# An attention kernel with image prompts: x turned by VectorE instead of TensorE, and another order of loads on SyncE's queue

## The chip, the core and the metric

The kernel runs on one core of one Trainium2 chip. A core has TensorE (PE) for matmuls, whose results go to eight PSUM banks, VectorE (DVE), ScalarE (ACT), GpSimd (POOL), and SyncE (SP), which here does nothing but issue DMAs, one after the other in program order. Sixteen DMA engines carry them. All data are float32. The metric is the time of one execution on the device in microseconds (us); the median of some timed executions stands for a kernel.

## The reference, cut to what matters

```python
# x (8, 112, 320), ehs (8, 375, 512): the last 4 tokens of ehs are image prompts
text_ehs, ip_ehs = ehs[:, :-4], ehs[:, -4:]              # 371 and 4 tokens
q, k_t, v_t = heads(x @ W_q), heads(text_ehs @ W_k), heads(text_ehs @ W_v)   # 20 heads of 16
probs_t  = softmax(einsum('bhsd,bhtd->bhst', q, k_t) * scale)
text_out = einsum('bhst,bhtd->bhsd', probs_t, v_t)
qsem = l2norm(einsum('bhst,bte->bhse', probs_t, text_ehs))     # wide: 512 per head
sem  = einsum('bhse,bne->bhsn', qsem, l2norm(ip_ehs))
fused = einsum('bhsd,bhnd->bhsn', q, heads(ip_ehs @ W_k_ip)) * scale + 0.5 * sem
probs_ip = softmax(fused) * smask[:, None]
out = (text_out + einsum('bhsn,bhnd->bhsd', probs_ip, heads(ip_ehs @ W_v_ip))) @ W_out + b_out + x
```

## The kernel before, in words

The 8 batches have 20 heads each, taken in 5 groups of 4. A step (b, g) is one group of one batch, and 40 steps follow one another, (0,0) to (7,4); a loop (L1207 on) writes out 35 of them, and the last batch has its own loop. `qsem` is never formed: its norm comes from a Gram matrix of the context, so that one product of the probabilities with a matrix `u` (Gram matrix, values and prompt columns side by side) gives all that a head needs.

One step of the main loop, by engine:

- PE: `multiplied` (L735 to 756), 96 matmuls with 32 contraction rows, probabilities against `u`, into four PSUM banks `ps_qd`, one for each head (L748). Between them stand the scores of the step two ahead (L686): two heads before the first matmul ("now") and two at the seventh row tile ("then"). The step is filled up by `between(b, g)` (L1079 to 1129): the next batch's Gram matrix (L502), values (L578) and keys (L544), queries (L315 to 358), and the projection of the finished batch (`ps_a` L950, `ps_o` L962).
- DVE: the maximum of each score row (L709), the transposition of the probabilities for the next step, 128x1536, from xg to xgT (`transposed`, L729), the context's transposition ct to ctxT (L404, three of 128x512 per batch), and `reduced` (L794), which multiplies `ps_qd` by the probabilities and sums; it reads a bank last, so the next step's matmuls into that bank wait for it.
- ACT: the exponential (L712), the copies of prompt logits (L714), of value sums (L761), and those of keys (L540, L551) and values from PSUM.
- POOL: the u of the next step from `vr` (L655) and smaller products.
- SP: the queue of DMAs. Each of the four heads' probabilities goes from p to xg, 162.3 KB (`sent`, L721); the Gram matrix goes to u in twelve pieces (`gram_to_groups`, L520), the values through DRAM to vr (L594, L603). Bulk loads stand in the same queue: the context of batch b+3 at the end of step (b,4) (`load_next`; four blocks of 176.0 KB, L140, and four rests of 9.5 KB, L145), the prompt values vip at the same place (L611, 560 KB), x as kept for the residual, x_sb, in three loads at the ends of steps (0,0), (1,0) and (2,0) (L1178), w_out at (0,2), and a copy of prompt values by head from DRAM to DRAM, vipx, at (5,1) (L618). The issue of a DMA waits until the engine's data are ready and until the eighth DMA before it has landed, as eight semaphores go round.

Queries are made for one batch (0), for pairs (1 and 2, 3 and 4, 5 and 6) and for one (7). `project_queries` turns x (112 x 320 per batch) by three PE transposes per batch (L333) into PSUM, ACT copies them to xT (L336), nine matmuls with wq follow in three pieces (L344), and DVE multiplies them by a mask into qm (L353). The transposes of a pair are run as one block at (0,1), (1,3), (3,3) and (5,3), the three pieces of matmuls in later steps. In the last step before a pair's turn, `turned` makes the "now" scores come after the first block's start, since they need the new qm.

Of the kernel before, what the change touches and what calls it, by code (L numbers as in the profile page):

```python
# [8 lines left out]
F32 = mybir.dt.float32  # L9
# [11 lines left out]
def kernel(  # L21
# [76 lines left out]

    x_sb = const.tile([S, B, C], F32, tag="x_sb", name="x_sb")
    wq_sb = const.tile([P, NC, CP], F32, tag="wq_sb", name="wq_sb")  # L100
    wk_sb = const.tile([P, NE, CP], F32, tag="wk_sb", name="wk_sb")
# [9 lines left out]
    sm_sb = const.tile([S, 1], F32, tag="sm_sb", name="sm_sb")  # L111
    bias_sb = const.tile([S, C], F32, tag="bias_sb", name="bias_sb")

    def load_channels(eng, t, w):
# [14 lines left out]
    def chunk(t, e):  # L129
        return t.rearrange("t (p e) -> t e p", e=NE)[:, e, :]  # L130

    def load_ctx(b):
        ct = io.tile([P, NT, E], F32, tag="ct", name=f"ct_{b}")
        if b >= LEAD:

            v = ct.rearrange("p c e -> p (c e)").rearrange("p (j f) -> p j f", f=P)
            full = TT // RG
            nc.gpsimd.memset(v[:, full, :], 0.0)
            for a in range(QN):
                nc.sync.dma_start(  # L140
                    v[a * RG : (a + 1) * RG, :full, :],
                    ehs[b, : full * RG, a * P : (a + 1) * P].rearrange("(j i) f -> i j f", i=RG),
                )
            for a in range(QN):
                nc.sync.dma_start(  # L145
                    v[a * RG : a * RG + TT - full * RG, full, :],
                    ehs[b, full * RG : TT, a * P : (a + 1) * P],
                )
            return v
# [8 lines left out]
    loaded = {0: load_ctx(0)}  # L158
    nc.scalar.dma_start(ip_sb, ehs[:, TT:, :])

# [154 lines left out]
    def project_queries(bs):  # L315
        n = len(bs)
        end = bs[0] == B - 1
        xT = work.tile([P, NC, 2 * S], F32, tag="xT", name=f"xT_{bs[0]}", bufs=1)
# [5 lines left out]
        nc.gpsimd.memset(xT[REST:, FULL, :], 0.0)  # L324
        for i in range(NC):
            cn = min(P, C - i * P)
            if bs[0] == 0:

                ps = ps_qd.tile([P, 512], F32, tag="qd", name=f"ps_x_0_{i}")
            else:  # L330
                ps = bank(f"ps_x_{bs[0]}_{i}", spare=i > 0)
            for j, b in enumerate(bs):
                nc.tensor.transpose(  # L333
                    ps[:cn, j * S : (j + 1) * S], x_sb[:, b, i * P : i * P + cn], ident[:S, :S]
                )
            nc.scalar.copy(xT[:cn, i, : n * S], ps[:cn, : n * S])  # L336
            yield
        for i in range(NC):
# [4 lines left out]
            for j in range(NC):  # L343
                nc.tensor.matmul(  # L344
                    ps[:, : n * S],
                    wq_sb[:, j, i * P : (i + 1) * P],
                    xT[:, j, : n * S],
                    start=(j == 0),
                    stop=(j == NC - 1),
                )  # L350
# [164 lines left out]

    def gram_to_groups(b, blocks, eng=nc.sync):

        for q in blocks:
            for a in range(GROUP):
                eng.dma_start(  # L520
                    st[b]["u"][a * RG : (a + 1) * RG, q * GW : (q + 1) * GW],
                    ug[q * RG : (q + 1) * RG, :],
                )
# [411 lines left out]
    def prompt_sums_and_projection(b, s, eng, part, n, h0, i0, i1, w, attn, ah):  # L935
# [11 lines left out]

        ps = bank(f"ps_a_{b}_{h0}")
        for i in range(i0, i1):
# [129 lines left out]
    def between(b, g):  # L1079
# [16 lines left out]
        if g == 1:  # L1096
            if new:
                run(("v", nb), lambda: values(nb), 1 if b == 0 else 2)
            if b == 0:
                run(("pp",), prompt_projections)  # L1100
            for bs in first if b == 0 else ():
                run(("q", bs[0]), lambda: project_queries(bs), 3)
        if g == 2 and new:
# [6 lines left out]
        if g == 3:  # L1110
            if new:
                run(("k", nb), None, 1)
            if b > 0 and new:
                run(("f", b - 1), None)
            for bs in first if b > 0 else ():
                run(("q", bs[0]), lambda: project_queries(bs), 3)
            for bs in rest:
                run(("q", bs[0]), None)
        if g < NT and nb + 1 < B:
            run(("c", nb + 1), lambda: transposed_context(nb + 1))  # L1120
        if g == 4:
            if b > 0 and new:
# [3 lines left out]
            for bs in (first if b > 0 else []) + (rest if b < B - 2 else []):  # L1126
                run(("q", bs[0]), None)
            if b == 0:
                run(("t", b), lambda: prompt_logits(b))

# [22 lines left out]
    nc.gpsimd.tensor_copy(wv_sb[:, :, C:], wk_sb[:, :, FULL * P : C])  # L1153
    spread(nc.gpsimd, wk_sb)
    run(("q", 0), None)
    run(("k", 0), lambda: keys(0))
# [4 lines left out]
    drain(transposed_context(1))  # L1161
    run(("q", 0), None)
    run(("k", 0), None)
    for a in range(GROUP):
# [15 lines left out]
    def load_rest(n):  # L1180

        if n == 0:
            load_x(1, 3)
        elif n == 2:
            load_channels(nc.sync, wo_sb, w_out)
        elif n == 3:
            nc.sync.dma_start(sm_sb, smask.unsqueeze(1))
            nc.sync.dma_start(bias_sb, b_out.partition_broadcast(S))
        elif n == NG:
            load_x(3, 5)  # L1190
        elif n == 2 * NG:
            load_x(5, B)


    def ahead(n):
# [11 lines left out]
    for n, (b, g) in enumerate(steps[:-NG]):  # L1207
        now, more, then = ahead(n)
        turned = (b, g) == (0, 2) or g == NG - 1 and any(bs[0] == b + 2 for bs in pairs)
        if not turned:  # L1210
            for c, a in now:
                scores(*c, a)
                probabilities(*c, a)
        for j, _ in enumerate(multiplied(b, g)):
            if j == 0:
                for c, a in now if turned else ():
                    scores(*c, a)
# [7 lines left out]
            if j == 2:  # L1225
# [5 lines left out]
                if 1 <= g <= 3:  # L1231
                    gram_to_groups(b + 1, {1: (0,), 2: (2,), 3: (3,)}[g])

# [173 lines left out]
```

## Time and profile before

| | us |
|---|---|
| median of 3 timed executions | 427.46 (427.1 to 427.54) |
| the profiled execution, its own time | 429.28 |
| its span, first to last instruction | 427.6 |

| engine | busy, share of the span |
|---|---|
| ACT | 188.7 us, 44% |
| POOL | 110.9 us, 26% |
| DMA queue of SP and ACT | 58.5% of 16 engines' time, 62.42 MB |

The profile is that of one execution. A row of the timeline has the start in us from the span's start, the duration (of a row "xN", of N like instructions from the first start to the last end), engine, line, operation, output and input tile, and in brackets how long the engine had been idle before and what released it. A row of the waits has engine, tile and line of the instruction that waited, what it waited for, and then us in total, times, and the longest. A row of a line's forms has the least, median and greatest duration in ns.

### The profile page before, as it was taken

To read this page: it belongs to the slowest core of one execution; us is meant where nothing else is said; L and a number is where in the kernel's file an instruction comes from. 1 tells how busy PE (TensorE), PEld (TensorE's weight loads), DVE (VectorE), ACT (ScalarE), POOL (GpSimd) and SP (SyncE) were. 2 spreads that over 40 slices of the span, in tenths; PEclk is the share of its full clock that TensorE was granted. 3 is DMA by queue.
4 is the path that set the end of the run, shared out by engine and by line. 5 is a ranking of instruction groups with operands and counts; after the bars stand their busy time and mean duration, and the time that the engine had idled before them with its cause. 6 is when DMAs were issued, how large, how long until landed. Compare 5 with 4: busy or idle time off the path is not lost.

```text
span 427.6 us, 13996 instructions
## 1 busy us (share of the span) xinstructions
PE 417.4 (98%) x5521; PEld 326.8 (76%) x5521; DVE 327.4 (77%) x672; ACT 188.7 (44%) x659; POOL 110.9 (26%) x275
## 2 busy tenths in 40 slices
PE   7999999999999999999999999999999999999995
PEld 7867767887767867788777877779776987777993
DVE  5038569887987869897896979797877887888873
ACT  2344342245433443436335363334533373446773
POOL 5310101112061112511151120611143120505550
PEclk9999999999999999999999999999999999999999
DMA  8677665687655956567556956458556537564200
GB/s 252 189 191 210 152 159 156 161 203 150 163 142 140 204 136 175 142 145 173 151 136 140 189 124 186 132 130 177 140 165 149 151 102 184 148 151 116 69 3 27
DMA packets 57631, 64.28 MB, mean 150 GB/s; under 512 B 18448, under 2 KB 51592, under 8 KB 57566
## 3 DMA queue, kind: packets, MB, share of 16 engines
q1 hardware_dynamic: 56934, 62.42, 58.5%
q8 instruction: 44, 0.72, 0.8%
q10 hardware_dynamic: 632, 0.96, 0.7%
q14 instruction: 21, 0.17, 0.1%
HBM read 18.67 MB, written 5.32 MB: 56 GB/s over the span
## 4 chain that ended last, share of the span: by engine, by line
PE 83%; DMA 5%; DVE 5%; ACT 4%; issue 1%; SPq 1%; POOL 0%; DVEq 0%; ACTq 0%
PE ps_qd L748 36%; PE ps_v L578 12%; PE ps_k L544 9%; PE ps_s L686 9%; PE ps_g L502 6%; PE ps_q L344 3%; DMA xg<-p 3%; PE ps_o L962 3%; DMA vipx<-vipd 2%; DVE xgT L729 1%; PE ps_g L458 1%; ACT p L712 1%; ACT shared L787 1%; DMA ip_sb<-in_ctx_dram 1%; PE ps_x L333 1%
## 5 line engine op out<-in xcount | busy, mean ns | idle before, releaser
L748 PE MATMUL ps_qd<-u,xgT 32*112 32x168 f32 (+11 forms) x3840 | 219.9, 351 | 0.3 <-POOL u L655 0.3
L748 PEld LDWEIGHTS ps_qd<-u,xgT 32*112 32x112 f32 x3840 | 187.2, 172 | 27.1 <-DVE ss L794 1.3
L729 DVE STREAM_TRANSPOSE xgT<-xg 128x1536 f32<-128x1536 f32 (+1 forms) x45 | 119.5, 2674 | 18.2 <-DMA xg<-p 17.5
L712 ACT ACTIVATE p<-ps_s,nmx 112x371 f32<-112x371 f32 x156 | 85.2, 587 | 65.9 <-DVE nmx L709 45.2
L709 DVE TENSOR_REDUCE nmx<-ps_s 112x1 f32<-112x371 f32 x160 | 77.2, 527 | 26.6 <-PE ps_s L686 24.6
L794 DVE CUSTOM_DVE_ANT_0 junk<-ps_qd,p 112x371 f32<-112x371 f32 x146 | 79.3, 543 | 17.9 <-PE ps_qd L748 1.4
L686 PE MATMUL ps_s<-kT,qm 32*112 32x375 f32 (+1 forms) x320 | 66.4, 496 | 0.7 <-DVE qm L353 0.6
L655 POOL COPY u<-vr 128x64 f32<-128x64 f32 x120 | 26.0, 238 | 149.9 <-PE ps_qd L748 99.2
L578 PE MATMUL ps_v<-wv_sb,ctxT 128*128 128x384 f32 (+1 forms) x192 | 63.0, 477 | 0.0
L578 PEld LDWEIGHTS ps_v<-wv_sb,ctxT 128*128 128x128 f32 x192 | 35.7, 190 | 20.9
L761 ACT COPY pvs<-ps_qd 112x21 f32<-112x21 f32 x151 | 16.3, 190 | 74.4 <-PE ps_qd L748 74.1
L544 PE MATMUL ps_k<-ctxT,wk_sb 128*128 128x371 f32 x136 | 46.9, 488 | 0.2 <-DVE ctxT L425 0.2
L544 PEld LDWEIGHTS ps_k<-ctxT,wk_sb 128*128 128x128 f32 x136 | 24.4, 189 | 14.0 <-issue 0.5
L686 PEld LDWEIGHTS ps_s<-kT,qm 32*112 32x112 f32 x320 | 23.8, 170 | 12.7 <-issue 10.3
L502 PE MATMUL ps_g<-ctxT 128*32 128x375 f32 (+11 forms) x672 | 30.4, 333 | 0.0
L502 PEld LDWEIGHTS ps_g<-ctxT 128*32 128x32 f32 x672 | 27.7, 110 | 2.0
L585 ACT COPY vext<-ps_v 128x384 f32<-128x384 f32 (+1 forms) x24 | 11.3, 471 | 31.9 <-PE ps_v L578 31.8
L353 DVE TENSOR_SCALAR qm<-ps_q,emask 128x224 f32<-128x224 f32 (+1 forms) x25 | 9.0, 395 | 20.3 <-PE ps_q L344 20.2
L714 ACT COPY ipl<-ps_s 112x4 f32<-112x4 f32 x140 | 24.4, 174 | 0.0
L937 POOL TENSOR_TENSOR wv<-vip,w 112x1280 f32<-112x1280 f32 x6 | 14.8, 2470 | 28.2 <-DVE w L877 28.2
L404 DVE STREAM_TRANSPOSE ctxT<-ct 128x512 f32<-128x512 f32 x18 | 20.1, 1119 | 1.8 <-DMA ct<-in_ctx_dram 1.8
L475 POOL TENSOR_TENSOR ug<-ug,half 128x128 f32<-128x128 f32 (+1 forms) x24 | 10.5, 449 | 32.1 <-ACT ug L474 32.1
(171 smaller groups left out, 320.2 us busy)
## 6 DMA issues: line engine op xcount, KB each, us to landing
xg<-p SPq DMA_DIRECT2D x156, 162.3 KB
u<-ug SPq DMA_DIRECT2D x124, 99.0 KB
ct<-in_ctx_dram SPq DMA_DIRECT2D x24, 176.0 KB
vr<-vd SPq DMA_DIRECT2D x32, 120.0 KB
vip<-vipd SPq DMA_DIRECT2D x6, 560.0 KB
vd<-vext SPq DMA_DIRECT2D x7, 320.0 KB
vd<-vext SPq DMA_DIRECT2D x7, 160.0 KB
out_dram<-ob SPq DMA_DIRECT2D x8, 140.0 KB
```

The lines of the kernel that those rows point to most:

```text
L404: nc.vector.transpose(ctxT[:, :, c * P : (c + 1) * P].rearrange("p e (j i) -> p j e i", i=RG), ct[:, some, :].rearrange("p j (k e) -> p j ...
L502: nc.tensor.matmul(ps[c][q * RG : (q + 1) * RG, j * RG - c * P : T - c * P], ctxT[:, e, j * RG : (j + 1) * RG], ctxT[:, e, j * RG : T], st ...
L544: nc.tensor.matmul(ps[:, :TT], wk_sb[:, e, i * P : (i + 1) * P], s["ctxT"][:, e, :TT], start=(e == 0), stop=(e == NE - 1),)
L578: nc.tensor.matmul(ps[:, :w], ctxT[:, e, c * P : (c + 1) * P], wv_sb[:, e, :w], start=(e == 0), stop=(e == NE - 1),)
L655: nc.gpsimd.tensor_copy(v, dealt(b, c, s["vr"][:, c * QN : (c + 1) * QN, g, :]))
L686: nc.tensor.matmul(ps[:S, :w], qm[a * RG : (a + 1) * RG, i, r, j * S : (j + 1) * S], s["kT"][a * RG : (a + 1) * RG, i, :w], start=True, st ...
L709: nc.vector.tensor_reduce(nmx, ps[:S, :TT], AX.X, ALU.max, negate=True)
L712: nc.scalar.activation(s["p", g][:, a, :], ps[:S, :TT], AF.Exp, bias=nmx)
L714: nc.scalar.copy(s["ipl"][:, groups[g][a], :], ps[:S, TT:T])
L729: nc.vector.transpose(xT[:, j : j + n].rearrange("p j (k q) -> p q j k", q=QN), xg[:, :, j * RG : (j + n) * RG].rearrange("p q (j k) -> p ...
L748: nc.tensor.matmul(banks[a][:S, j * RG : UW], xT[a * RG : (a + 1) * RG, j, :S], region(b, c)[a * RG : (a + 1) * RG, q, j * RG - c * P :], ...
L794: nc.vector.tensor_tensor_reduce(out=junk, in0=ps[:S, :TT], in1=s["p", g][:, a, :], scale=1.0, scalar=0.0, op0=ALU.mult, op1=ALU.add, accu ...
```

## The change

It touches what turns x, and where loads stand in SP's queue.

- x of batches 1 to 7 is loaded a second time, in blocks (xr_sb; four DMAs per batch, each 28 partitions with 4 pieces of 320 bytes), and turned by DVE: three stream transposes per batch over a stride of 5 columns, straight into xT. PE transposes and ACT copies stay for batch 0. The channels come out in another order, so wq is loaded a second time, in the prologue behind batch 0's queries, in row order (p c) instead of (c p), and spread again.
- x is turned at (0,0) and (0,1) for batches 1 and 2, and at (1,2), (1,3), (3,2), (3,3), (5,2) for the others, after that step's reductions and context transposition. The context transposes of batch 2 move from (0,0), (0,1), (0,2) to (0,1), (0,2), (0,3).
- `turned` goes; only at (0,3) do the "now" scores come behind the first block (`late`). The transposed heads of odd batches get a bank of the scores' pool; prompt_logits of batch 0 moves from behind (0,4) to behind its value sums.
- Loads: context 2 moves from the prologue to the end of (0,0); 3 and 4 stay; 5, 6 and 7 move from the ends of (2,4), (3,4), (4,4) into (2,0), (3,0), (4,0), blocks between the "now" and the "then" probabilities, rests behind the "then" ones. x_sb is loaded batch by batch at (b,4). The blocks xr stand at the ends of (0,0) and (1,0), between the probabilities of (1,0), and in (2,4) and (4,4). w_out goes to (1,1), vipx to (6,0). The pieces of u go in halves, spread over the middles and ends of steps (b,1), (b,2), (b,3).

```diff
+    def load_pairs(eng, t, w):
+        w = w.rearrange("(p c) f -> p c f", c=5)
+        eng.dma_start(t[0::2, :, :C], w[:, :3, :])
+        eng.dma_start(t[1::2, :2, :C], w[:, 3:, :])
+
+    def load_x_blocks(b, j):
+        for a in range(QN):
+            nc.sync.dma_start(
+                xr_sb[a * RG : a * RG + S // QN, j, :, :XB],
+                x[b, :, a * XB : (a + 1) * XB].rearrange("(q i) f -> i q f", q=QN),
+            )
...
+        for j in range(n if qT is None else 0):
+            for e in range(NC):
+                nc.vector.transpose(
+                    xT[:, e, j],
+                    xr_sb[:, j, :, e : e + XB]
+                    .rearrange("p q (m c) -> p q m c", c=5)[:, :, :, 0:4:3],
+                )
             yield
...
-        ps = bank(f"ps_a_{b}_{h0}")
+        ps = bank(f"ps_a_{b}_{h0}", spare=b % 2 == 1)
...
-        if g < NT and nb + 1 < B:
+        if nb + 1 < B and g in ((1, 2, 3) if b == 0 else (0, 1, 2)):
             run(("c", nb + 1), lambda: transposed_context(nb + 1))
+        for bs in first:
+            if g in ((0, 1) if b == 0 else (2, 3)[: len(bs)]):
+                run(("q", bs[0]), lambda: project_queries(bs))
...
+    nc.gpsimd.memset(wq_sb[:, FULL, :], 0.0)
+    load_pairs(nc.sync, wq_sb, w_q)
+    load_x_blocks(1, 0)
     run(("k", 0), None)
...
-    load_next(2)
...
+    spread(nc.gpsimd, wq_sb)
     prologue.close()
...
-        if n == 0:
-            load_x(1, 3)
-        elif n == 2:
-            load_channels(nc.sync, wo_sb, w_out)
-        elif n == 3:
+        if n == 3:
...
-        elif n == NG:
-            load_x(3, 5)
-        elif n == 2 * NG:
-            load_x(5, B)
+        elif n == NG + 1:
+            load_channels(nc.sync, wo_sb, w_out)
+        if g == NG - 1:
+            load_x(b, b + 1 if b < B - 2 else B)
+    x_loads = {
+        (0, 0): ((0, 0), (2, 1)),
+        (1, 0): ((3, 0), (4, 1)),
+        (2, NG - 1): ((5, 0), (6, 1)),
+        (4, NG - 1): ((7, 0),),
+    }
...
-        turned = (b, g) == (0, 2) or g == NG - 1 and any(bs[0] == b + 2 for bs in pairs)
-        if not turned:
+        late = (b, g) == (0, NG - 2)
...
                 if 1 <= g <= 3:
-                    gram_to_groups(b + 1, {1: (0,), 2: (2,), 3: (3,)}[g])
+                    gram_to_groups(b + 1, {1: (0,), 2: (1,), 3: (3,)}[g], parts=halves[g == 2])
+                elif g == 0 and 2 <= b < B - 3:
+                    load_ctx_blocks(b + 3)
+                for c, i in x_loads.get((b, g), ())[: int(n > 0)]:
+                    load_x_blocks(c, i)
...
+        if n == NG - 1:
+            run(("t", b), lambda: prompt_logits(b))
...
-        if g == NG - 1:
+        if n == 0:
+            load_next(2)
+        elif g == NG - 1 and b < 2:
             load_next(b + 3)
+        elif g == 0 and 2 <= b < B - 3:
+            load_ctx_rest(b + 3)
+        for c, i in x_loads.get((b, g), ())[1:]:
+            load_x_blocks(c, i)
         if g == 1:
-            gram_to_groups(b + 1, (1,))
+            gram_to_groups(b + 1, (0,), parts=halves[1])
+            gram_to_groups(b + 1, (1,), parts=halves[0])
+        elif g == 2:
+            gram_to_groups(b + 1, (2,))
         elif g == 3:
+            gram_to_groups(b + 1, (3,), parts=halves[1])
             values_to_groups(b + 1)
...
-        if (b, g) == (B - 3, 1):
+        if (b, g) == (B - 2, 0):
             prompt_values_by_head()
```

More of the change, by code (lines that the diff above doesn't have):

```diff
@@ L514, in gram, with gram_to_groups @@
             yield
-    def gram_to_groups(b, blocks, eng=nc.sync):
+    def gram_to_groups(b, blocks, eng=nc.sync, parts=range(GROUP)):
         for q in blocks:
-            for a in range(GROUP):
+            for a in parts:
                 eng.dma_start(
@@ L1154 @@
     spread(nc.gpsimd, wk_sb)
+    nc.gpsimd.memset(xr_sb, 0.0)
     run(("q", 0), None)
@@ L1180, in load_rest @@
     def load_rest(n):
[L1182 to L1186 removed]
+        if n == 3:
             nc.sync.dma_start(sm_sb, smask.unsqueeze(1))
             nc.sync.dma_start(bias_sb, b_out.partition_broadcast(S))
[L1189 to L1192 removed]
+        elif n == NG + 1:
[8 more added lines that the diff above has]
+    }
+    halves = (range(GROUP // 2), range(GROUP // 2, GROUP))
     def ahead(n):
@@ L1208 @@
         now, more, then = ahead(n)
-        turned = (b, g) == (0, 2) or g == NG - 1 and any(bs[0] == b + 2 for bs in pairs)
-        if not turned:
-            for c, a in now:
-                scores(*c, a)
-                probabilities(*c, a)
+        late = (b, g) == (0, NG - 2)
+        for c, a in now if not late else ():
+            scores(*c, a)
+            probabilities(*c, a)
         for j, _ in enumerate(multiplied(b, g)):
             if j == 0:
-                for c, a in now if turned else ():
+                for c, a in now if late else ():
                     scores(*c, a)
```

71 lines of the change are left out of this document (38 added, 33 removed).

## The prediction

> **What bounds the kernel now.** I read the page first: its busy shares, and the chain that ended last.
>
> ```profile
> span 427.6 us, 13996 instructions
> ```
>
> ```profile
> PE 417.4 (98%) x5521; PEld 326.8 (76%) x5521; DVE 327.4 (77%) x672; ACT 188.7 (44%) x659; POOL 110.9 (26%) x275
> ```
>
> ```profile
> PE 83%; DMA 5%; DVE 5%; ACT 4%; issue 1%; SPq 1%; POOL 0%; DVEq 0%; ACTq 0%
> ```
>
> TensorE (PE) is busy for 417.4 of 427.6 us. There are two ways to be faster: less work on PE, or less of the little that PE waits. And whatever slows PE's suppliers, VectorE (DVE) at 77% and the DMAs, counts only where it reaches PE. So I read next PE's waits, then DVE's.
>
> ```profile
> PE ps_x L333 <- ACT kT L551: 1.4, 3, 0.9
> ```
>
> ```profile
> PE ps_q L344 <- ACT kT L551: 0.8, 3, 0.3
> ```
>
> ```profile
> PE ps_s L686 <- DVE qm L353: 0.6, 1, 0.6
> PE ps_ip L665 <- ACT kT L540: 0.3, 1, 0.3
> ```
>
> ```profile
> DVE xgT L729 <- DMA xg<-p: 17.5, 10, 3.8
> ```
>
> Of PE's waits 1.4 + 0.8 + 0.6 + 0.3 = 3.1 us stand at the queries' projection (L333, L344) and at the two instructions behind it; the change touches all four. DVE's 17.5 us are the probabilities' way through the DMA queue: ten times it waits for xg, once for 3.8 us. The queue is full just there, in the windows view (the last two columns are the DMA share and GB/s):
>
> ```profile
> 139.00:146.00 7.00, 7.00 (x147) 6.57 (x143) 6.54 (x15) 3.51 (x15) 0.71 (x3) 1.00 0.99 204
> ```
>
> **The change part by part.** All differences are made against this execution: it took 429.28 us, its span is 427.6, so 1.7 us lie around the span and stay. The median of the timed runs is 427.46; I take the differences off that. Steps are written (batch, group).
>
> 1. *x of batches 1 to 7 leaves PE.* The rows of the line and of the places:
>
> ```profile
> L333 PE MATMUL ps_x<-ident,x_sb x24: 257/259/316, 16.0 to 327.0; 112*128 112x112 f32 x16, 112*64 112x112 f32 x8
> ```
>
> ```profile
> 59.69 0.79 PE L333 MATMUL ps_x<-ident,x_sb 112*128 112x112 f32 x6
> 60.41 0.93 PE L748 MATMUL ps_qd<-u,xgT 32*112 32x392 f32 x8
> ```
>
> ```profile
> 227.50 0.80 PE L333 MATMUL ps_x<-ident,x_sb 112*128 112x112 f32 x6 [0.27 <-ACT kT L551]
> 228.23 1.22 PE L748 MATMUL ps_qd<-u,xgT 32*112 32x392 f32 x10
> ```
>
> ```profile
> 326.76 0.51 PE L333 MATMUL ps_x<-ident,x_sb 112*128 112x112 f32 x3 [0.87 <-ACT kT L551]
> 327.19 0.58 PE L748 MATMUL ps_qd<-u,xgT 32*112 32x392 f32 x2
> ```
>
> Of 24 transposes 21 go. Six cost PE 60.41 - 59.69 = 0.72 us at (0,1) and 228.23 - 227.50 = 0.73 at (3,3), as six do at (1,3), and three cost 327.19 - 326.76 = 0.43 at (5,3). That is 2.6 us of PE. With them go the waits ahead, 0.27 twice and 0.87 once (L333's 1.4). ACT's twelve copies go too, at no gain, since ACT is at 44%.
>
> DVE takes 21 stream transposes of 128x128. No row has that size, two have neighbours:
>
> ```profile
> L404 DVE STREAM_TRANSPOSE ctxT<-ct x18: 1091/1113/1182, 47.4 to 317.1; 128x512 f32<-128x512 f32 x18
> ```
>
> ```profile
> L729 DVE STREAM_TRANSPOSE xgT<-xg x45: 1534/2972/3043, 33.5 to 407.2; 128x1536 f32<-128x1536 f32 x35, 128x768 f32<-128x768 f32 x10
> ```
>
> From 512 to 1536 columns the time grows by (2972 - 1113) / 1024 = 1.82 ns per column, which leaves 0.18 us for 0 columns: 0.41 us for 128. Bounds: 0.28 (a quarter of the 1.113 us for 512) and 0.56 (twice that, for the strided reads). I take 0.4, 1.2 us per batch. Whether PE's gain arrives is read where they run, after the reduction of (1,2) and (3,2):
>
> ```profile
> 219.74 1.00 DVE L709 TENSOR_REDUCE nmx<-ps_s 112x1 f32<-112x371 f32 x2 [0.17 <-PE ps_s L686]
> ```
>
> ```profile
> 227.06 0.08 DVE L794 DVE_READ_ACCUMULATOR2_ANT ss<- 112x1 f32 x1
> ```
>
> Between these two rows DVE works throughout; 0.17 us ahead of the first is its only gap. The second ends the last reduction of (3,3), at 227.14, and frees the fourth PSUM bank. PE begins the next step at 228.23 and needs that bank 0.4 us later (term 5 shows it), at 228.6: 1.5 us of room. PE would come 0.73 + 0.27 = 1.0 earlier and DVE 1.2 - 0.17 = 1.0 later, 2.0 in all: 0.5 too much, so 0.5 of the 1.0 would arrive at (3,3), and a little less where the second batch's turn, in the next step, is late too. I take **-0.4 at (1,3) and -0.4 at (3,3)** (ends: -1.0 with DVE free, +0.2 if a transpose takes 0.56 and both turns are late). The Trainium skill, "VectorE: DVE Perf Modes", section "Rules for kernel authors", speaks against this part: 128x128 is to be transposed on TensorE where a PSUM destination will do, as it did here, and section "The three transpose paths" adds that VectorE turns 32x32 blocks only, which the regrouped loads and weights are for. Its figures for bf16 are 390 ns on TensorE and 311 on VectorE; an estimate by them is 21 x 0.39 = 8.2 us off PE, where the rows, with 259 ns and transposes that overlap, give 2.6.
>
> 2. *Spare bank for ps_a.* In batches 2, 4 and 6 the first query matmul waits as here; the three make the 0.8 us of L344.
>
> ```profile
> 177.88 1.40 PE L344 MATMUL ps_q<-xT,wq_sb 128*128 128x224 f32 x6 [0.27 <-ACT kT L551]
> ```
>
> The transposed heads get a bank of the scores' pool, so kT's copy is no longer ahead: **-0.8** (ends -0.8 and 0; the scores' pool could be late instead).
>
> 3. *Batch 0.* The 0.72 us of (0,1), the 0.64 behind qm and the 0.30 of ps_ip go, 1.66 in all, as x is turned by DVE, the first scores are no longer held back behind qm, and the prompt's logits move to behind the sums. What is late next: DVE, which has this gap in (0,4):
>
> ```profile
> 80.32 0.81 DVE L353 TENSOR_SCALAR qm<-ps_q,emask 128x224 f32<-128x224 f32 x2 [0.96 <-PE ps_q L344]
> ```
>
> A context transpose of 1.1 us (L404) moves to (0,3), ahead of it; the gap pays for 0.96, and 0.15 us would be left. I take **-1.4** (-1.7 with DVE free, to 1.1 - 1.66 = -0.5 with the gap gone for another reason).
>
> 4. *vipx one step later, and batch 7's part at (5,3).*
>
> ```profile
> SPq L721 <- DMA vipx<-vipd: 1.9, 1, 1.9
> ```
>
> ```profile
> 321.84 2.99 DVE L729 STREAM_TRANSPOSE xgT<-xg 128x1536 f32<-128x1536 f32 x1 [2.45 <-DMA xg<-p]
> ```
>
> The DRAM copy held SP for 1.9 us; xg landed late, DVE waited 2.45, and PE the 0.87 of above. With the copy away from that step both 0.87 and 0.43 go: **-1.3** (to -0.4, if DVE's turn of batch 7 takes PE's place). At its new place, (6,0), SP has neither a context nor vip to load: I take 0.
>
> 5. *Second context load at (2,0).* ct_5's blocks go between the two pairs of xg of that step, while ct_4 and vip are still under way. SP's rows, and what follows:
>
> ```profile
> ct<-in_ctx_dram SPq DMA_DIRECT2D x24, 176.0 KB
> ```
>
> ```profile
> 137.25 1.85 SPq L140 DMA_DIRECT2D ct<-in_ctx_dram  x4
> 139.14 1.30 SPq L145 DMA_DIRECT2D ct<-in_ctx_dram  x4
> 140.86 0.32 SPq L611 DMA_DIRECT2D vip<-vipd  x1
> 142.22 3.56 SPq L721 DMA_DIRECT2D xg<-p  x4
> ```
>
> ```profile
> 152.71 2.98 DVE L729 STREAM_TRANSPOSE xgT<-xg 128x1536 f32<-128x1536 f32 x1 [3.82 <-DMA xg<-p]
> ```
>
> ```profile
> 159.07 0.08 DVE L794 DVE_READ_ACCUMULATOR2_ANT ss<- 112x1 f32 x1
> ```
>
> ```profile
> 157.71 0.68 PE L748 MATMUL ps_qd<-u,xgT 32*112 32x392 f32 x2
> ```
>
> ```profile
> 158.13 1.65 PE L748 MATMUL ps_qd<-u,xgT 32*112 32x392 f32 x8
> ```
>
> Here DVE is late already. From the transpose's start to the end of the last reduction are 6.4 us, to 159.15. PE begins the step with two banks at 157.71 and takes the others 0.42 later, at 158.13, where it crawls: it is held for about 1 us, until the fourth is free. Four blocks more are 0.70 MB, 3.45 us at the window's 204 GB/s, ahead of the second pair. Against it: SP had issued the pairs by 145.78, and 6.9 us passed to xgT's start, which the 0.56 MB of vip ahead and its slowest engine explain in part; some of the new bytes pass in that time. I take half, **+1.8** (0 to +4.0: all hidden, or all of 3.45 and one more issue of 0.46). Gained in return is nothing: the contexts of 6 and 7 leave (3,4) and (4,4), behind which PE waits for no bank in its list.
>
> 6. *Blocks of x of batch 3 between the xg pairs of (1,0), and x_sb by batch.* xgT of (1,2) waits already:
>
> ```profile
> 102.49 2.96 DVE L729 STREAM_TRANSPOSE xgT<-xg 128x1536 f32<-128x1536 f32 x1 [2.10 <-DMA xg<-p]
> ```
>
> Four issues at 0.46 us (1.85 / 4, as ct's) hold the second pair 1.85 us, and 0.14 MB at 204 GB/s are 0.7 more. With 6.4 us behind 102.49, the last reduction ends at 108.9, so PE at (1,2) has no more slack than at (2,1)'s edge. About half falls in time in which SP waits for ACT's exponentials anyway: **+1.0** (0 to +2.5). The Trainium skill, "DMA: Bandwidth & Descriptors", section "Specifications", asks for pieces of 512 B and more for full rate; these have 320 B. An estimate by it: at twice their weight the 0.14 MB take 0.7 us more; no row here shows that apart.
>
> 7. *Tail.* The halves of u put two issues ahead of vr at (6,3):
>
> ```profile
> 371.86 2.48 SPq L520 DMA_DIRECT2D u<-ug  x4
> ```
>
> ```profile
> 383.09 0.59 POOL L655 COPY u<-vr 128x64 f32<-128x64 f32 x3 [10.08 <-DMA vr<-vd]
> ```
>
> ```profile
> 384.12 1.22 PE L748 MATMUL ps_qd<-u,xgT 32*112 32x392 f32 x9
> ```
>
> The copies end at 383.68, 0.4 us before PE begins (7,0). Two issues of 0.62 are 1.2 later, but SP waits there for ACT's exponentials and may catch up part: **+0.3** (0 to +1.2).
>
> Hidden, taken at nothing: wq's second load and spreading in the prologue (POOL is busy 26%), smaller halves of u, wo and the rest of x_sb (no one waits for them before the next batch).
>
> Sum: -0.4 - 0.4 - 0.8 - 1.4 - 1.3 + 1.8 + 1.0 + 0.3 = **-1.2 us**, 426.3. Ends: -1.0 - 1.0 - 0.8 - 1.7 - 1.3 = -5.8; 0.2 + 0.2 + 0 - 0.5 - 0.4 + 4.0 + 2.5 + 1.2 = +7.2.
>
> **The rivals.**
>
> *The loads cost more than PE gains* (slower). Mechanism: the second xg pair of (2,0) lands behind ct_4, vip and ct_5. It decides from a start of xgT (2,2) at 151.7 us in before's time, 1.0 ahead of the row; each us later is one of PE's. With all 3.45 us of bytes ahead, +4.0 instead of +1.8, and +2.0 at (1,0): 429.5. For it: a DMA share of 0.99. Against: the first pair and vip land as before.
>
> *No load reaches PE* (faster). Terms 5 and 6 are 0, since more than vip's time hides them: -2.8 further, 423.5; with DVE free at (1,3) and (3,3) as well, 422.3. For it: of DVE's ten waits for xg, 17.5 us, PE's list shows next to nothing. Against: the one of 3.82 did cost PE.
>
> *DVE takes PE's place*, and the change gives its own gain back: turning x costs each of DVE's tight steps 1.2 us, so -0.4 twice becomes +0.2 twice, and batch 0 gives -0.9: 428.0. The skill's rule named above would have it so. For it: 0.17 us of idle; against: 1.5 us of room at (3,3).
>
> **How the numbers follow.** Forecast (424.9 to 427.6) 0.41; slower by the loads 0.26; no load reaches PE 0.22; DVE 0.11. A measurement here tells apart about 0.2%, 0.86 us: same is 426.6 to 428.3. Faster: 0.22 and 0.26 of the forecast, 0.48; same: 0.15 of the forecast and 0.07 of DVE's, 0.22; slower: the rest, 0.30. With cases of both signs the forecast's own range is 424.9 to 427.6; the range of 8 in 10 reaches into both load cases, 421.8 to 430.3, and leaves out the far thirds of them.
>
> **What would show it.** Right: no L333 on PE after the prologue, L344's waits on kT gone, 21 DVE transposes near 0.4 us; (5,3)'s xgT without its 2.45 us. xgT(2,2)'s start tells term 5: against the steps' starts, 1 to 2.5 us later than before my sum stands, no later the fast rival, 3 and more the slow one. A wait of PE on ss at (1,4) or (3,4) is DVE's rival. Wrong altogether: a long wait for xr, wq or ct on DVE or PE, which I have at nothing.

## The result and the profile after

The changed kernel takes 424.7 us (median of 13 timed executions, 422.69 to 429.36) against 427.79 (427.0 to 428.18) beside it: a ratio of 0.9928, 95% interval 0.9909 to 0.9947. The ratio leaves out two of the 13 executions, 429.22 and 429.36, which ran in a slower state. That is 3.1 us faster, where 1.2 was forecast. The profiled execution took 425.05 us, its span is 423.3, so again 1.7 us lie around it. The span of before's execution was 4.3 us longer, but that execution had been 1.5 us over its median and this one 0.35: the traces show more than the medians do. Before was profiled only once, so what is read below against it may contain up to about 1.5 us that belongs to that execution.

The page of the changed kernel, in the same three lines as before:

```profile
span 423.3 us, 14029 instructions
...
PE 415.8 (98%) x5500; PEld 327.2 (77%) x5500; DVE 330.8 (78%) x693; ACT 185.6 (44%) x647; POOL 111.6 (26%) x277
...
PE 92%; DVE 3%; ACT 2%; DMA 1%; issue 0%; POOL 0%; DVEq 0%; POOLq 0%
```

PE's share of the chain has gone from 83% to 92%: of what stood between PE's instructions a good part is gone. PE's waits in full (lines have moved, L748 is L784, L344 L380, L729 L765, L794 L830):

```profile
PE ps_w L470 <- POOL ident masks.py:199: 1.5, 1, 1.5
PE ps_wT L1081 <- DVE w_last L1076: 0.8, 1, 0.8
PE ps_qd L784 <- POOL u L691: 0.3, 1, 0.3
PE ps_k L580 <- DVE ctxT L461: 0.2, 1, 0.2
PE ps_s L722 <- ACT ipl L750: 0.2, 1, 0.2
```

All four waits at the queries (3.1 us) are gone; what is left belongs to the start, the end and three small places. DVE waits as long for the probabilities as before, but its longest wait has grown from 3.8 to 4.9 us:

```profile
DVE xgT L765 <- DMA xg<-p: 16.5, 10, 4.9
```

To see where the time went I measure a step from its first ps_qd matmul to that of the next. Of 36.88 us ahead of step (0,0) nothing changed. Sums of steps in us, each from one profiled execution ("again" is a second one of the changed kernel, the columns from e1 on are the experiments):

| steps | before | changed | again | e1 | e2 | e3 | e5 | e6 | e7 | e8 | e10 | e4 | e11 |
|---|---|---|---|---|---|---|---|---|---|---|---|---|---|
| (0,1), (0,2) | 21.75 | 19.75 | 19.75 | 19.75 | 21.02 | 19.75 | 19.75 | 19.75 | 19.75 | 20.19 | 19.75 | 19.75 | 19.75 |
| (0,3) to (1,0) | 26.93 | 27.59 | 27.32 | 27.82 | 27.37 | 27.36 | 27.33 | 27.36 | 27.33 | 34.48 | 27.58 | 27.32 | 28.52 |
| (1,1), (1,2) | 21.35 | 21.46 | 21.38 | 22.24 | 21.54 | 21.35 | 21.99 | 21.35 | 21.52 | 21.35 | 21.35 | 21.93 | 22.34 |
| (1,3), (1,4) | 18.04 | 17.64 | 17.74 | 17.83 | 18.04 | 17.80 | 18.51 | 21.15 | 17.75 | 16.97 | 16.99 | 17.79 | 17.83 |
| (2,0) | 9.63 | 9.63 | 9.63 | 9.63 | 9.63 | 9.63 | 9.63 | 11.39 | 9.63 | 9.63 | 9.63 | 9.63 | 9.63 |
| (2,1), (2,2) | 22.22 | 23.27 | 23.76 | 21.35 | 24.80 | 25.93 | 23.38 | 21.35 | 21.35 | 21.35 | 21.35 | 21.35 | 21.35 |
| (2,3) | 10.01 | 9.49 | 9.49 | 9.49 | 9.49 | 10.01 | 9.49 | 9.49 | 9.49 | 9.49 | 9.49 | 9.49 | 9.49 |
| (3,1), (3,2) | 21.35 | 21.35 | 21.35 | 23.40 | 21.35 | 21.35 | 21.35 | 21.35 | 21.35 | 21.73 | 21.35 | 21.35 | 21.49 |
| (3,3), (3,4) | 18.04 | 16.97 | 16.97 | 17.07 | 18.04 | 16.97 | 18.26 | 16.97 | 16.97 | 17.07 | 16.97 | 16.97 | 17.08 |
| (4,3) | 10.01 | 9.49 | 9.49 | 9.49 | 9.49 | 10.01 | 9.49 | 9.49 | 9.49 | 9.49 | 9.49 | 9.49 | 9.49 |
| (5,1), (5,2) | 21.35 | 21.73 | 22.04 | 22.01 | 21.35 | 21.35 | 21.67 | 21.66 | 21.35 | 21.35 | 21.35 | 21.35 | 21.88 |
| (5,3), (5,4) | 18.92 | 16.54 | 16.54 | 16.64 | 17.33 | 16.54 | 17.14 | 16.54 | 16.54 | 16.54 | 16.54 | 18.68 | 16.67 |
| (6,3), (6,4) | 17.92 | 17.39 | 17.40 | 17.40 | 17.40 | 17.91 | 17.40 | 17.40 | 17.43 | 17.40 | 17.40 | 17.65 | 17.40 |

Down to (7,0) the changed kernel is 342.06 us long where before's 347.24: 5.2 us less. The last batch takes 1.0 us longer in this execution and 43.4 us, as before, in the second. So the gains are 2.0 at (0,1) and (0,2), 2.4 at (5,3) and (5,4), 1.1 at (3,3), 1.6 at (2,3), (4,3) and (6,3) together, 0.4 at (1,3); the losses 0.4 to 0.7 around (0,4), 1.1 to 1.5 at (2,1) and (2,2), 0.4 to 0.7 at (5,1).

Where x is turned, after the last reductions of (3,2) and (3,3) on DVE:

```profile
217.71 1.11 DVE L440 STREAM_TRANSPOSE ctxT<-ct 128x512 f32<-128x512 f32 x1
218.74 0.71 DVE L368 STREAM_TRANSPOSE xT<-xr_sb 128x128 f32<-128x128 f32 x3
219.36 0.97 DVE L745 TENSOR_REDUCE nmx<-ps_s 112x1 f32<-112x371 f32 x2
...
226.50 0.08 DVE L830 DVE_READ_ACCUMULATOR2_ANT ss<- 112x1 f32 x1
226.50 0.73 DVE L368 STREAM_TRANSPOSE xT<-xr_sb 128x128 f32<-128x128 f32 x3
```

and the line's forms, least, median and greatest:

```profile
L368 DVE STREAM_TRANSPOSE xT<-xr_sb x21: 273/284/320, 47.5 to 316.2; 128x128 f32<-128x128 f32 x21
```

Three take 0.6 to 0.7 us one behind another, not 1.2. PE at the same place:

```profile
225.68 0.45 PE L986 MATMUL ps_a<-ident,attn 112*128 112x112 f32 x3
226.06 0.57 PE L722 MATMUL ps_s<-kT,qm 32*112 32x375 f32 x2
226.08 0.58 PE L784 MATMUL ps_qd<-u,xgT 32*112 32x392 f32 x2
226.47 0.48 PE L722 MATMUL ps_s<-kT,qm 32*112 32x375 f32 x2
226.50 0.80 PE L784 MATMUL ps_qd<-u,xgT 32*112 32x392 f32 x6
```

The last reduction's row ends at 226.58. The third and fourth of PE's ps_qd matmuls, which take the last two banks, stand in the row that starts at 226.50. The two meet within 0.1 us, and PE has no named wait there: DVE just keeps up.

Around (2,0), on SP and on DVE:

```profile
139.37 0.32 SPq L647 DMA_DIRECT2D vip<-vipd  x1
140.05 2.85 SPq L757 DMA_DIRECT2D xg<-p  x2
142.95 2.06 SPq L157 DMA_DIRECT2D ct<-in_ctx_dram  x4
145.11 2.47 SPq L757 DMA_DIRECT2D xg<-p  x2
```

```profile
152.14 2.97 DVE L765 STREAM_TRANSPOSE xgT<-xg 128x1536 f32<-128x1536 f32 x1 [4.88 <-DMA xg<-p]
```

Step (2,1) begins at 145.36, so xgT of (2,2) starts 6.8 us into it, where in before 152.71 - 146.99 = 5.7: 1.1 us later, and PE lost that.

### The profile page after: what moved, and what is told of

It reads as the page before. It is cut to its first block, busy times and chain, and to the rows that moved or that the text cites. A ratio compares the mean times of both kernels' runs of the same rounds, so it can differ in the third digit from the quotient of the medians.

```text
span 423.3 us, 14029 instructions
## 1 busy us (share of the span) xinstructions
PE 415.8 (98%) x5500; PEld 327.2 (77%) x5500; DVE 330.8 (78%) x693; ACT 185.6 (44%) x647; POOL 111.6 (26%) x277
## 4 chain that ended last, share of the span: by engine, by line
PE 92%; DVE 3%; ACT 2%; DMA 1%; issue 0%; POOL 0%; DVEq 0%; POOLq 0%
PE ps_qd L784 39%; PE ps_v L614 13%; PE ps_k L580 11%; PE ps_s L722 10%; PE ps_g L538 7%; PE ps_q L380 3%; PE ps_o L998 3%; PE ps_g L494 1%; DMA xg<-p 1%; PE ps_w L470 1%; ACT shared L823 1%; DVE xgT L765 1%; DVE nmx L745 1%; DVE junk L830 1%; PE ps_k L596 1%; PE ps_c L453 1%
## 5 line engine op out<-in xcount | busy, mean ns | idle before, releaser
L784 PE MATMUL ps_qd<-u,xgT 32*112 32x168 f32 (+11 forms) x3840 | 220.3, 351 | 0.3 <-POOL u L691 0.3
L784 PEld LDWEIGHTS ps_qd<-u,xgT 32*112 32x112 f32 x3840 | 189.0, 172 | 26.3 <-DVE ss L830 1.1
L765 DVE STREAM_TRANSPOSE xgT<-xg 128x1536 f32<-128x1536 f32 (+1 forms) x45 | 119.7, 2678 | 18.8 <-DMA xg<-p 16.5
L748 ACT ACTIVATE p<-ps_s,nmx 112x371 f32<-112x371 f32 x156 | 85.0, 586 | 67.5 <-DVE nmx L745 58.7
L830 DVE CUSTOM_DVE_ANT_0 junk<-ps_qd,p 112x371 f32<-112x371 f32 x146 | 79.2, 543 | 17.8 <-PE ps_qd L784 1.4
L691 POOL COPY u<-vr 128x64 f32<-128x64 f32 x120 | 25.9, 238 | 143.0 <-PE ps_qd L784 85.8
```

The lines of the kernel that those rows point to most:

```text
L691: nc.gpsimd.tensor_copy(v, dealt(b, c, s["vr"][:, c * QN : (c + 1) * QN, g, :]))
L748: nc.scalar.activation(s["p", g][:, a, :], ps[:S, :TT], AF.Exp, bias=nmx)
L765: nc.vector.transpose(xT[:, j : j + n].rearrange("p j (k q) -> p q j k", q=QN), xg[:, :, j * RG : (j + n) * RG].rearrange("p q (j k) -> p ...
L784: nc.tensor.matmul(banks[a][:S, j * RG : UW], xT[a * RG : (a + 1) * RG, j, :S], region(b, c)[a * RG : (a + 1) * RG, q, j * RG - c * P :], ...
L830: nc.vector.tensor_tensor_reduce(out=junk, in0=ps[:S, :TT], in1=s["p", g][:, a, :], scale=1.0, scalar=0.0, op0=ALU.mult, op1=ALU.add, accu ...
```

## The experiments

Each experiment ran beside before again, on one of three chips. Before's median was 427.4 to 427.9 us there, so kernels of different groups are best compared by their ratios to it.

### Undone one at a time: contexts, turning, bank

**e1**, contexts 5 to 7 back at the ends of (2,4), (3,4), (4,4):

```diff
-                elif g == 0 and 2 <= b < B - 3:
-                    load_ctx_blocks(b + 3)
...
-        elif g == NG - 1 and b < 2:
+        elif g == NG - 1:
             load_next(b + 3)
-        elif g == 0 and 2 <= b < B - 3:
-            load_ctx_rest(b + 3)
```

> The changed kernel with one part undone: contexts 5, 6 and 7 load again at the ends of steps (2,4), (3,4), (4,4). Theory A (the second context load at (2,0) costs PE about 1 us, as xgT of (2,2) lands late behind its 0.70 MB): step (2,1) goes back from 11.56 to about 10.7 us, DVE's wait there from 4.9 to 3.8, and the time falls from 424.7 by 0.8 to 1.1 to about 423.7. Rival (the load passes in vip's time; the longer step has another cause): (2,1) stays at 11.5 and the time at 424.7 within 0.3. Rival two (the load is worth its new place): waits of 1.5 to 2 us come back at (3,1) and (4,1) and reach PE, 425.5 or more.

Measured: 426.53 us (423.51 to 428.88), ratio 0.9966 [0.9943, 0.9989]. Theory A holds for the step and not for the time, 423.7: (2,1) and (2,2) fall to 21.35 us, 1.9 to 2.4 below the changed kernel's and even 0.9 below before's. But (3,1) and (3,2) rise by 2.05, so rival two holds there: the load is worth its new place, given what else now stands at the old one. At (4,1), which it named too, nothing changed (10.72). SP's queue in e1 shows this:

```profile
186.72 1.93 SPq L157 DMA_DIRECT2D ct<-in_ctx_dram  x4
188.69 1.30 SPq L167 DMA_DIRECT2D ct<-in_ctx_dram  x4
190.31 2.31 SPq L127 DMA_DIRECT2D xr_sb<-in_x_dram  x4
192.66 1.18 SPq L647 DMA_DIRECT2D vip<-vipd  x1
193.94 3.54 SPq L757 DMA_DIRECT2D xg<-p  x4
```

```profile
202.58 2.96 DVE L765 STREAM_TRANSPOSE xgT<-xg 128x1536 f32<-128x1536 f32 x1 [5.04 <-DMA xg<-p]
```

The blocks of x of batch 6 have come between context and vip, the probabilities follow at 193.94, and DVE waits 5 us.

**e2**, x turned by PE and ACT with all other orders of the changed kernel. The edit puts before's `project_queries` and its calls back, takes xr_sb and wq's second load out, restores `turned` (with (0,3) held back as well) and loads x_sb in before's three pieces.

> The changed kernel with x of batches 1 to 7 turned by PE and ACT again (no blocks of x, no second wq, x_sb in three loads as before, and the held-back scores of before), all other loads and orders as in the changed kernel. Theory A (the gain is PE's own work and the waits ahead of it): 0.7 at (0,1), 1.0 at (1,3) and (3,3) and 0.5 to 1.0 at (5,3) come back, 3.2 to 3.7 us, so about 428, no faster than before. Rival (the order of the loads made the gain, and DVE's turning gives its own back): 424.5 to 425.5.

Measured: 429.52 us (428.56 to 429.86), ratio 1.0044 [1.0031, 1.0057]. At the places of the turning come back 1.27 us at (0,1) and (0,2), 0.40 at (1,3), 1.07 at (3,3), 0.79 at (5,3), 3.5 in all, as theory A has it; the rest is at (2,1) and (2,2), 1.5 longer, with context 5 there and x_sb in one piece of 420 KB. By the medians the other orders without the turning on DVE are slower than before, so it is the turning that decides whether the change pays. They are not all losses: the bank, the logits and vipx gain here too (e3, e11, e4), and against them stand the 2.6 us that (2,1) and (2,2) lose against before. Down to (7,0) this trace is even 0.7 shorter than before's, whose execution was 1.5 over its median. Of the 2.0 us of (0,1) and (0,2), 0.73 stay gone; the "now" scores of (0,3) still come behind the first block here, so part of that gain is in the scores' order.

**e3**, the bank of the transposed heads:

```diff
-        ps = bank(f"ps_a_{b}_{h0}", spare=b % 2 == 1)
+        ps = bank(f"ps_a_{b}_{h0}")
```

> The changed kernel with the transposed heads of odd batches in the matmul pool's banks again. Theory A (the 0.3 us waits of the query matmuls at (2,3), (4,3), (6,3), and as much of PE that the rows do not call a wait, go with the bank): each of these steps is 0.4 to 0.5 longer again, 1.2 to 1.5 us in all, 426.0. Rival (they went with the turning or the loads): 424.7 within 0.3, no wait of L380 on kT.

Measured: 426.37 us (425.04 to 428.37), ratio 0.9977 [0.9962, 0.9993]. (2,3), (4,3) and (6,3) are 0.52 us longer each. PE in e3 and then in the changed kernel:

```profile
179.03 0.45 PE L986 MATMUL ps_a<-ident,attn 112*128 112x112 f32 x3
179.76 1.40 PE L380 MATMUL ps_q<-xT,wq_sb 128*128 128x224 f32 x6 [0.27 <-ACT kT L587]
```

```profile
176.57 0.45 PE L986 MATMUL ps_a<-ident,attn 112*128 112x112 f32 x3
176.87 1.31 PE L380 MATMUL ps_q<-xT,wq_sb 128*128 128x224 f32 x6
```

From the heads' transposes to the first query matmul are 0.73 us against 0.30. Of these 0.43 the profile names 0.27 as a wait; the other 0.16 stand where the changed kernel's queries begin, 0.15 before the modelled end of the transposes. The last 0.09 of the 0.52 are in the row of the queries, 1.40 against 1.31. Theory A holds.

### The queue: which loads may stand together

**e6**, context 4 at the end of (1,3) instead of (1,4):

```diff
-        elif g == NG - 1 and b < 2:
+        elif (b, g) in ((0, NG - 1), (1, NG - 2)):
             load_next(b + 3)
```

> The changed kernel with context 4 loaded at the end of (1,3) instead of (1,4), so that it no longer meets vip and context 5. Theory A (the queue around (2,0) is what makes (2,1) and (2,2) long, 11.56 and 11.71 against 10.72 and 10.63): xgT of (2,2) starts 2 to 4 us earlier, both steps go to 10.7, 1.9 us gained, 422.8, less up to 0.5 for a later xgT of (2,0). Rival (the jam only moves, to (1,4), whose bank has 0.15 us to spare): (1,4) or (2,0) gets 1 us longer, 424.2 or more.

Measured: 427.21 us (426.15 to 430.76), ratio 1.0006 [0.9984, 1.0029]. The rival holds: (2,1) and (2,2) are clean at 21.35, and (1,4) and (2,0) are 3.6 and 1.8 us longer. The load stood ahead of vr, and POOL and PE waited for it, which theory A had not seen:

```profile
138.84 0.59 POOL L691 COPY u<-vr 128x64 f32<-128x64 f32 x3 [13.23 <-DMA vr<-vd]
```

```profile
PE ps_qd L784 <- POOL u L691: 3.0, 2, 2.8
```

**e9**, the changed kernel again.

> The changed kernel without an edit, profiled a second time beside the others. The one-bank kernel, alike in its loads, had 12.53 and 13.40 us at (2,1) and (2,2) where the changed one had 11.56 and 11.71. Theory J (the queue around (2,0) has contexts 4 and 5 and vip in flight and lands xgT of (2,2) differently in each execution): every step but (1,1), (2,1), (2,2), (3,1), (5,1) repeats within 0.1 us, and one of these differs by 0.5 or more; the times spread over 3 us again. Rival (the spread is of PE or spread over all steps): these steps repeat within 0.2 and others differ.

Measured: 424.94 us (423.79 to 425.89), ratio 0.9925 [0.9905, 0.9944]. (2,1) took 12.05 us instead of 11.56, (5,1) 11.41 instead of 11.10; beside them (0,3) to (1,0), 27.32 instead of 27.59, (1,3), and (6,0), 9.89 instead of 9.75, differ by 0.1 or more, all in stretches with bulk loads, and so does the last batch, 43.41 instead of 44.40, with the last load of x_sb near its start. The times spread over 2.1 us. Theory J holds in its second half: a step that it named, (2,1), differs by 0.49. Its first half does not hold, since steps that it had not named differ too.

**e7**, contexts back as in e1 and the blocks of x away from them:

```diff
-        (2, NG - 1): ((5, 0), (6, 1)),
-        (4, NG - 1): ((7, 0),),
+        (3, 0): ((5, 0), (6, 1)),
+        (5, 0): ((7, 0),),
```

> Contexts 5 to 7 at the ends of (2,4), (3,4), (4,4) as before the change, and the blocks of x of batches 5 and 6 at (3,0), of 7 at (5,0), away from them. Theory A (a step is late where a context, vip and the blocks of x stand in the queue together: (2,1) in the changed kernel, (3,1) and (3,2) with 11.69 and 11.71 us in the kernel with the contexts back): (2,1), (2,2), (3,1), (3,2), (5,1) all near 10.7, so 2.0 us under the changed kernel's steps, 422.5, and a narrower spread of times. Rival (the context at (2,4) alone makes (3,1) late now that x_sb is loaded there too): (3,1) stays above 11.3, 424.5.

Measured: 423.46 us (422.05 to 423.71), ratio 0.9879 [0.9859, 0.9899]. Every step from (2,0) to (6,4) is, within 0.05 us, as short as in any of the runs; the last batch takes 44.71 us, the longest of all runs and 1.3 more than the shortest, for a cause that was not looked for. By the ratios the gain on the changed kernel is 0.5%, near 2 us; by the medians it is 1.2; the times lie within 1.7 us. Theory A holds, short of its 422.5: xgT starts at 149.91 us in (2,1) and at 198.90 in (3,1), with waits that reach no bank:

```profile
149.91 2.98 DVE L765 STREAM_TRANSPOSE xgT<-xg 128x1536 f32<-128x1536 f32 x1 [2.13 <-DMA xg<-p]
```

**e8**, as e7 and the blocks of batches 3 and 4 at (0,2):

```diff
-        (1, 0): ((3, 0), (4, 1)),
+        (0, 2): ((3, 0), (4, 1)),
```

> As the kernel with the blocks of x late, and the blocks of batches 3 and 4 at (0,2) instead of (1,0), so that only before's loads are left there. Theory A as for that kernel; the blocks at (1,0) are priced by the difference: my forecast had 1.0 us, the changed kernel's (1,1) and (1,2) show 0 to 0.1 in one execution and 0.7 to 0.9 in another with the same loads. So 0.1 to 0.9 us less than that kernel, 422, with (1,1) at 10.7. Rival (at (0,2) the blocks delay a xg of batch 0): (0,3) or (0,4) 0.3 or more longer, no gain.

Measured: 425.36 us (424.06 to 429.81), ratio 0.995 [0.9927, 0.9973]; the profiled execution took 429.81, the longest of them. Its (0,3) to (1,0) are 7.2 us longer than e7's, while (1,1) to (1,4) are at their shortest. The rival holds, and its 0.3 us was far too little for that execution. SP and DVE there:

```profile
64.30 1.92 SPq L630 DMA_DIRECT2D vd<-vext  x1
66.33 1.84 SPq L757 DMA_DIRECT2D xg<-p  x2
68.22 1.22 SPq L556 DMA_DIRECT2D u<-ug  x2
69.49 1.89 SPq L127 DMA_DIRECT2D xr_sb<-in_x_dram  x4
71.48 1.87 SPq L757 DMA_DIRECT2D xg<-p  x2
```

```profile
75.59 2.97 DVE L765 STREAM_TRANSPOSE xgT<-xg 128x1536 f32<-128x1536 f32 x1 [2.45 <-DMA xg<-p]
```

One issue of the values takes 1.92 us, where the changed kernel's takes 0.59; then the blocks stand for 1.89 between the pairs of probabilities. The second pair goes out at 71.48, in the changed kernel at 67.57, and DVE waits about 2.5 us in this step and in the two behind it. Single issues of 1.1 us and more stand in every trace, mostly elsewhere; why this one is long is open, and with it why other executions are shorter.

**e10**, as e7 and both blocks of x at the end of (1,0), behind the second pair of probabilities:

```diff
-                for c, i in x_loads.get((b, g), ())[: int(n > 0)]:
+                for c, i in x_loads.get((b, g), ())[: int(n > NG)]:
...
-        for c, i in x_loads.get((b, g), ())[1:]:
+        for c, i in x_loads.get((b, g), ())[int(n != NG) :]:
```

> The kernel with the contexts back and the blocks of x late, and the blocks of batch 3 at the end of (1,0), behind the second pair of probabilities instead of ahead of it. My forecast's theory (standing between the pairs holds the second pair up and costs about 1 us at (1,0) to (1,2)): these steps lose their excess, (1,0) 10.20 to 9.7, (1,2) 10.80 to 10.63, (1,3) 9.09 to 8.4, so 0.5 to 1.3 less, 422.5. Rival (the excess is that of the bulk behind (0,4), context 3, vip and x_sb, in before and after alike, and of DVE): no more than 0.2 less, or the blocks land too late for (1,2) and it is longer.

Measured: 421.77 us (420.96 to 422.11), ratio 0.9864 [0.9845, 0.9882], the lowest of all, though its interval overlaps e7's. What decides are the steps: (1,1) to (1,4) take 38.34 us instead of e7's 39.27, (1,0) is 0.5 shorter and (0,4) 0.7 longer. My forecast's theory holds for (1,0) to (1,4). SP in e10, where the four probabilities now go ahead of x:

```profile
92.61 3.54 SPq L757 DMA_DIRECT2D xg<-p  x4
96.20 1.97 SPq L127 DMA_DIRECT2D xr_sb<-in_x_dram  x4
```

In the changed kernel the second pair went out behind four issues of 1.95 us, from 96.13 on.

### The rest: DVE's room, vipx, logits

**e5**, every transpose of x on DVE done twice to the same place (the work is doubled, the values stay):

```diff
+                for _ in range(2):
                     nc.vector.transpose(
```

> The changed kernel with each of DVE's 21 transposes of x done twice, to the same place: 0.72 us more of DVE per batch. Theory D (DVE has no room left in the steps where x is turned; the bank's slack is -0.2, -0.1 and 0.3 at (1,3), (3,3), (5,3)): these lose 0.4 to 0.7 each, (1,4) and (0,1) or (0,2) 0.3 to 0.5, in all 1.8 to 2.8 us, 427. Rival (my forecast's room of 1.5 us is there): under 0.5 in all.

Measured: 430.21 us (428.12 to 432.3), ratio 1.0053 [1.0031, 1.0075]; the profiled execution is the shortest of them. (3,3) and (3,4) are 1.29 us longer, (1,3) and (1,4) 0.87, (5,3) 0.60: 2.8 us. Theory D holds at these three; (0,1) and (0,2), which it named too, stay at 19.75. DVE in e5 at (3,2):

```profile
219.94 1.78 DVE L369 STREAM_TRANSPOSE xT<-xr_sb 128x128 f32<-128x128 f32 x6
221.65 0.95 DVE L746 TENSOR_REDUCE nmx<-ps_s 112x1 f32<-112x371 f32 x2
```

1.71 us for six transposes instead of 0.62 for three go to the turning, and (3,3) is 0.79 longer at once. The medians differ by 5.5 us, the steps of the turning by 2.8; the rest was not placed.

**e4**, as e7 with vipx copied at (5,1) again:

```diff
-        if (b, g) == (B - 2, 0):
+        if (b, g) == (B - 3, 1):
             prompt_values_by_head()
```

> The kernel with the contexts back and the blocks of x late, and vipx copied at (5,1) again. Theory A (the copy holds SP and the probabilities behind it, and makes (5,3) and (5,4) late, also with nothing of x on PE): SP waits near 2 us for vipx, (5,3) and (5,4) get 0.6 and 1.0 longer, 9.0 and 9.2, so 1.3 to 1.7 us in all, 425.0. Rival (the turning on PE made (5,3) and (5,4) long, and its wait of 0.87 was for PSUM): both stay at 8.3 and 8.2, 423.5.

Measured: 424.67 us (423.72 to 427.26), ratio 0.994 [0.992, 0.9961]. (5,3) and (5,4) are 2.14 us longer than in e7, with nothing of x on PE: the copy makes them long, not the turning. But SP shows no wait for vipx here. In the trace the copy lands 6.7 us after its issue has ended and what follows in the queue 5 to 7 us after its own, where xg takes 2.1 us in an empty queue; DVE gets xg late, in the changed kernel it waits for nothing here (second row):

```profile
317.96 2.98 DVE L765 STREAM_TRANSPOSE xgT<-xg 128x1536 f32<-128x1536 f32 x1 [1.97 <-DMA xg<-p]
317.33 2.98 DVE L765 STREAM_TRANSPOSE xgT<-xg 128x1536 f32<-128x1536 f32 x1
```

and PE stalls inside its next step. Ahead of this row the profile names a wait of 0.31 us, inside it none; a step that does not stall has 48 such matmuls in 3.41 us:

```profile
322.94 4.60 PE L784 MATMUL ps_qd<-u,xgT 32*112 32x392 f32 x52
```

**e11**, as e7 with the prompt's logits behind (0,4)'s other work again:

```diff
-        if n == NG - 1:
-            run(("t", b), lambda: prompt_logits(b))
...
             for bs in (first if b > 0 else []) + (rest if b < B - 2 else []):
                 run(("q", bs[0]), None)
+            if b == 0:
+                run(("t", b), lambda: prompt_logits(b))
```

> The kernel with the contexts back and the blocks of x late, and the prompt's logits of batch 0 behind (0,4)'s other work again, as before the change. Theory A (PE's 0.30 us wait of ps_ip stands on the path): the wait comes back and (0,4) is 0.2 to 0.4 longer, 423.8. Rival (DVE's last reduction sets the start of (1,0), as its bank has no room): (0,4) and (1,0) together unchanged within 0.1, 423.5.

Measured: 424.02 us (422.81 to 425.06), ratio 0.991 [0.9891, 0.9929]. PE waits again, and longer than before the change:

```profile
PE ps_ip L701 <- ACT kT L576: 0.8, 1, 0.8
```

(0,3) to (1,0) are 1.2 us longer, the median 0.6. Theory A holds, since the wait is back and the stretch is longer than in any kernel without this edit but e8 (26.93 to 27.82). Its price is uncertain: 0.7 to 1.2 us by the steps, while the intervals of e11 and e7 overlap.

## Why the prediction was right, and where its sizes were off

The direction and the mechanism were right. The time, 424.7, lies in the wide range, 421.8 to 430.3, and 0.2 below the sum's own, 424.9 to 427.6. PE's own work and the four named waits went, and the queue at (2,0) gave a part back. The sum was 2 us short of the median and 3 to 4 short of the traces. As measured, the terms give -2.1 (1, with e10's 1.05 at (1,3)), -1.6 (2), -1.3 (3), -2.4 (4), +1.05 (5), +0.8 (6) and +0.4 at (5,1), together -5.2 as in the traces. By its terms:

1. *Turning x.* At (3,3) 1.07 us came instead of 0.4, the whole of PE's 0.73 and of the wait. The mis-sized number is DVE's transpose: 284 ns each and 0.6 to 0.7 us per batch against 0.4 and 1.2. By my own sum 0.7 - 0.17 + 1.05 = 1.6 us meet the 1.5 of room. That the room is used up is shown by e5. At (1,3) 0.4 came, as forecast, but by luck: e10 gets 1.05 there, so the blocks of term 6 took 0.65.
2. *Bank.* -1.57 instead of -0.8. I took the named wait of 0.27 for the cost; e3 shows 0.52 each, in the distance of the rows.
3. *Batch 0.* -2.0 and +0.66, together -1.34, where -1.4 was forecast. The match is partly luck. I had named 1.36 at (0,1) and (0,2), and 2.0 came: 1.27 are the turning (e2), 0.73 stay without it. Behind them I had 0.30 of gain and 0.15 of loss; +0.66 came, +0.39 in the second execution. The wait of ps_ip is part of it (e11); DVE at (0,4) and the load of x_sb were not told apart.
4. *vipx.* -2.38 instead of -1.3. I counted PE's named 0.87 and the three transposes; e4 shows that the copy costs 2.14 alone, and e2 that with it gone the turning on PE costs 0.79. The two overlapped in before: 2.14 + 0.79 = 2.93 is more than the 2.38 that came. The bound that I set, 1.3 as the most that two rows hold, was wrong, since a stall inside a row of matmuls is in no wait.
5. *Context 5.* +1.05 in one execution and +1.54 in another for +1.8: right in mechanism and place, and in size as far as it has one, for the same loads gave +1.16 in e5 and +3.71 in e3; xgT started 1.1 us later into its step, and I had put 1 to 2.5 as the sign of my sum. What I missed: context 4 alone costs nothing at (2,0) (21.35 in e1 and e7); before's own loss there, 0.87, came with x_sb's 420 KB behind it, which is not shown to be its cause, as no run takes that load alone out.
6. *Blocks of x at (1,0).* +0.76 by e10 against the changed kernel, (1,0) to (1,3), for +1.0. I placed it at (1,1) and (1,2); it showed at (1,3). No run varied the size of the pieces, so the 0.7 us that I estimated for 320 B remains untested.
7. *Tail.* Nothing of +0.3: (6,3) and (6,4) only gained. Issues added ahead of vr there found room.

Taken at nothing and mostly not nothing: (5,1), 0 (e3) to 0.7 us, where x of batch 7, x_sb and vip meet; e7 moves the first of them and has 21.35 again. Of the rivals, "DVE takes PE's place" was nearest to the truth in its mechanism: e5 shows that DVE has no room left in these steps. What kept it off is that a batch's turning takes 0.6 to 0.7 us and not 1.2. The rule of the Trainium skill that I set beside it, "VectorE: DVE Perf Modes", "Rules for kernel authors", 128x128 on TensorE, would have cost e2's 3.5 us at the places of the turning here, with PE the bound (98%) and DVE's share 77%. The loads' rival had the right place and too high a price. "No load reaches PE" is wrong for the changed kernel, by (2,1) and (2,2). With the loads moved, e7 and e10 come near to what it describes; that e10's 421.77 is close to its 422.3 is luck, as terms 2 and 4 were too small in it.

## What to carry to other kernels

When one engine is busy 98% of the time, as PE here, moving work off it to one at 77% can pay as long as each step still closes. That is counted from that step's rows and not from the shares: twice the work on DVE cost 2.8 us (e5).

In the one in-order DMA queue of this kernel the price of a bulk load was set by what else of bulk stood with it ahead of a small, needed transfer. Context, vip and the x_sb of one batch cost nothing measurable at (2,1) and (2,2) (21.35 us in e1 and e7); with context 5 as one more they took 23.3 to 25.9 us (the changed kernel, e5 and e3). A step of its own was not enough: a load that stood ahead of a needed transfer cost 5.4 us in e6 and was part of 7.2 in one execution of e8. Of the three places of x's blocks for batches 3 and 4, the one behind the step's last needed transfer was the cheapest (e10).

PE's waits in the profile were smaller here than what their cause took: 0.27 listed against 0.52 in the step (e3), and before's 0.87 at (5,3) against the 2.14 that the copy costs in e4. DVE's were the opposite: 16.5 us are listed for the probabilities, where all steps of the changed kernel down to (7,0) lose under 4 us against the shortest of any run. So measure the distance from step to step.

## What the runs showed that I had not expected

Transposes of 128x128 on DVE, with a stride of five columns in the source, start 0.21 to 0.25 us one behind another, 0.6 to 0.7 us for three, though one row alone shows 284 ns. A row of PE can hide a stall: 52 matmuls in 4.60 us (e4) are slower than 48 in 3.41 us in steps that do not stall, with no idle time named inside it. And the same program does not repeat where bulk loads meet: (2,1) and (2,2) together took 23.27 and 23.76 us in two executions of the changed kernel, 25.93 in e3, which has the same loads, while clean steps repeat to 0.01 us.
